# Cross-attention on one core: the score products split into column halves

## The chip, the cores and the metric

The kernel runs on one core of a Trainium2 chip. The metric is the device time of one execution in microseconds, from repeated executions on the same chip; the median is quoted. All data is 32-bit floating point.

The core has a matrix engine (PE in the profile, with PEld for the loads of its stationary operand), a vector engine (DVE), a scalar engine (ACT), a general engine (POOL) and a queue that issues transfers (SP). A product on PE holds up to 128 columns of one operand still in the array (the stationary operand, `lhsT`) while the columns of the other (the moving operand, `rhs`) stream past. The result lands in an accumulation memory, the PSUM, and several products can be summed there: the first has `start=True`, the last `stop=True`.

## The reference

For each of 64 batch items, `x` is 256 x 512 and `ctx` is 256 x 384:

```
text_p  = x   @ W_text  + b_text           # 256 x 512
audio_p = ctx @ W_audio + b_audio          # 256 x 512
Q = layer_norm(text_p,  g1, beta1)
K = layer_norm(audio_p, g2, beta2)
scores = Q @ K.T / sqrt(512)               # 256 x 256
alpha  = softmax(scores, axis=-1)
H = (alpha @ audio_p) @ W_out + b_out
out = layer_norm(H + x, g_out, beta_out)   # 256 x 512
```

The scores are the part that the change touches: 256 queries by 256 keys, each a sum over 512 hidden values.

## The kernel before

The work is staged as a software pipeline over the 64 items. The order of the instructions on each engine is the order in which the program text emits them; there is no scheduler. In one turn of the main loop (62 turns, `for b in range(B - 2)`) the kernel makes, in this order on PE: the scores of item `b`; the query projection of item `b + 2` (`ps_q`); the context product of item `b - 2`, or `alpha @ ctx` (`ps_z`); the key projection of item `b + 2` (`ps_k`); the output projection of item `b - 2` (`ps_y`). The projections use a scheme with seven block products instead of eight (class `Blocks`, line 487), so their moving operands are 256 columns wide as well. The last two items are finished after the loop in a shorter order, where the probabilities are turned on PE (`ps_e`, line 575) and the output is made with 512 columns (`ps_y`, line 639).

For the scores (method `scores` of class `Attention`, line 526), `qT` holds the normalised queries with the hidden dimension on the partitions, in `HC` = 4 chunks of 128; `kT` holds the keys in the same form. `LT` = 2 blocks of 128 queries are made one after the other. For each block, four products are summed into one 128 x 256 region of the PSUM tile `ps_sc`: the stationary operand is a 128 x 128 piece of `qT`, the moving operand is the 256-column chunk of `kT`. That is 8 products for an item.

Each product of 32-bit data stands in the trace as two pairs of records, a load of the stationary operand (LDWEIGHTS, on PEld) and the product itself (MATMUL, on PE): 64 items of 8 products are 1024 records of each kind for line 526. A transposition on PE (lines 183, 214, 227, 575) has 128 columns and stands as one pair.

Before the scores, ACT scales and shifts `qT` and `kT` chunk by chunk (method `affine`, line 458); the first product on each chunk waits for it. After them, DVE takes the row maxima from the whole of `ps_sc` (line 536) and ACT makes the exponentials from it (line 543).

Of the kernel before, what the change touches and what calls it, by code (L numbers as in the profile page):

```python
# [15 lines left out]
P = 128  # L16
# [6 lines left out]
def kernel(  # L23
# [41 lines left out]
    nc = tc.nc  # L65
    ctx.enter_context(tc.manual_schedule())
    B, L, D = x.shape
    S, DA = c.shape[1:]
    H = w_text.shape[1]
    LT, ST = L // P, S // P  # L70
    DC, AC, HC = D // P, DA // P, H // P
# [442 lines left out]
    class Attention:  # L514
# [4 lines left out]
        def scores(self, end=False):  # L519
            if end:  # L520
                self.sc = p_pj.tile([P, LT, S], F32, tag="pj", name="ps_sc")
            else:
                self.sc = p_at.tile([P, LT, S], F32, tag="at", name="ps_sc")
            for t in range(LT):
                for k in range(HC):
                    nc.tensor.matmul(  # L526
                        self.sc[:, t, :],
                        lhsT=self.qT[:, k, bass.ts(t, P)],
                        rhs=self.kT[:, k, :],
                        start=(k == 0),  # L530
                        stop=(k == HC - 1),
                    )

        def maxima(self):
            self.nmx = small.tile([P, LT], F32, tag="nmx", name="nmx")
# [239 lines left out]
    q, k, xT, cT = {}, {}, {}, {}  # L775
# [319 lines left out]
```

## Time and profile before

| what | value |
|---|---|
| median of 3 runs | 1415.37 us (1414.96 to 1416.03) |
| span of the profiled execution, first to last instruction | 1411.8 us |
| PE busy | 1403.2 us, 99% of the span, 6437 records |
| PEld busy | 1220.4 us, 86%, 6437 records |
| DVE, ACT, POOL busy | 87%, 66%, 62% |
| score products on PE (line 526) | 1024 records of 128x256, 231.5 us busy |
| loads for them (line 526) | 1024 records of 128x128, 194.6 us busy |
| mean granted clock of PE | 0.999 |

For the profiled execution only the span is on record as its own time; the timed runs' median lies 3.6 us above it.

How to read it: a MATMUL record runs from the moment in which the engine begins to fetch to a modelled end, so records of neighbouring products overlap and the mean duration of a record (379 ns for 256 columns) is not what a product costs in a stream. What it costs there is the distance between the starts of two neighbouring records, which is called the pitch below. The chain of waits shows this: it merges a run of records of one line into one piece, and the piece's length over the number of records is the pitch. A busy time in the groups is the union of the records' times, put down to each group once.

### The profile page before, as it was taken

To read this page: it belongs to the slowest core of one execution; us is meant where nothing else is said; L and a number is where in the kernel's file an instruction comes from. 1 tells how busy PE (TensorE), PEld (TensorE's weight loads), DVE (VectorE), ACT (ScalarE), POOL (GpSimd) and SP (SyncE) were. 2 spreads that over 40 slices of the span, in tenths; PEclk is the share of its full clock that TensorE was granted. 3 is DMA by queue.
4 is the path that set the end of the run, shared out by engine and by line. 5 is a ranking of instruction groups with operands and counts; after the bars stand their busy time and mean duration, and the time that the engine had idled before them with its cause. 6 is when DMAs were issued, how large, how long until landed. Compare 5 with 4: busy or idle time off the path is not lost.

```text
span 1411.8 us, 22761 instructions
## 1 busy us (share of the span) xinstructions
PE 1403.2 (99%) x6437; PEld 1220.4 (86%) x6437; DVE 1230.4 (87%) x1758; ACT 935.0 (66%) x2298; POOL 871.0 (62%) x1294
## 2 busy tenths in 40 slices
PE   9999999999999999999999999999999999999998
PEld 5888888888888888888888888888888888888885
DVE  6888898898888988988988889889889888898887
ACT  4667667676676676676766766766767667667663
POOL 5556666656656666666566566666665665666645
PEclk9999999999999999999999999999999999999999
DMA  8798877888888887787887887877888888878763
GB/s 211 206 259 229 245 233 218 246 232 224 241 243 219 232 233 228 234 226 237 231 230 235 225 238 232 231 232 232 221 243 237 222 240 239 222 235 232 223 212 125
DMA packets 450437, 322.32 MB, mean 228 GB/s; under 512 B 154885, under 2 KB 382981, under 8 KB 450310
## 3 DMA queue, kind: packets, MB, share of 16 engines
q1 hardware_dynamic: 450214, 320.72, 80.3%
q8 instruction: 52, 0.85, 0.3%
q14 instruction: 75, 0.61, 0.2%
q10 hardware_dynamic: 96, 0.13, 0.0%
HBM read 203.83 MB, written 116.92 MB: 227 GB/s over the span
## 4 chain that ended last, share of the span: by engine, by line
PE 98%; DVE 1%; POOL 1%; DMA 0%; ACT 0%; issue 0%; DVEq 0%; ACTq 0%
PE ps_q L487 27%; PE ps_k L487 21%; PE ps_y L487 20%; PE ps_sc L526 15%; PE ps_z L592 12%; PE ps_wao L252 1%; PE ps_y L639 1%; PE ps_q L374 0%; PE ps_k L374 0%; DMA c<-in_ctx_dram 0%; DVE yr L499 0%; PE ps_rows L214 0%; POOL yr L608 0%; POOL x L772 0%; DVE kr L499 0%; PE ps_wa L227 0%
## 5 line engine op out<-in xcount | busy, mean ns | idle before, releaser
L499 DVE TENSOR_TENSOR qr<-ps_q,qr 128x512 f32<-128x512 f32 x252 | 174.3, 692 | 88.9 <-PE ps_q L487 86.1
L526 PE MATMUL ps_sc<-kT,qT 128*128 128x256 f32 x1024 | 231.5, 379 | 0.0
L353 POOL TENSOR_SCALAR ve<-var 128x2 f32<-128x2 f32 x126 | 43.4, 344 | 290.0 <-ACT junk L392 289.8
L526 PEld LDWEIGHTS ps_sc<-kT,qT 128*128 128x128 f32 x1024 | 194.6, 190 | 26.9 <-issue 0.5
L543 ACT ACTIVATE e<-ps_sc,nmx 128x256 f32<-128x256 f32 x128 | 59.4, 468 | 230.3 <-DVE nmx L536 230.3
L608 POOL TENSOR_TENSOR yr<-yr,x 128x512 f32<-128x512 f32 x124 | 155.7, 1277 | 70.8 <-DVE yr L499 70.8
L499 DVE TENSOR_TENSOR kr<-ps_k,kr 128x512 f32<-128x512 f32 x252 | 174.4, 692 | 22.5 <-DVE kr L499 0.9
L487 PE MATMUL ps_q<-wtsum,xsum 128*128 128x256 f32 x756 | 193.7, 379 | 0.0
L499 DVE TENSOR_TENSOR yr<-ps_y,yr 128x512 f32<-128x512 f32 x248 | 171.6, 692 | 21.7 <-DVE yr L499 0.5
L487 PE MATMUL ps_k<-wa,cT 128*128 128x256 f32 x630 | 177.1, 379 | 0.0
L592 PE MATMUL ps_z<-eT,c 128*128 128x256 f32 x768 | 176.2, 379 | 0.0
L487 PE MATMUL ps_y<-wao,zT 128*128 128x256 f32 x620 | 174.1, 379 | 0.0
L355 POOL TENSOR_TENSOR rstd<-ve,nhalf 128x2 f32<-128x2 f32 x192 | 157.3, 819 | 16.0
L592 PEld LDWEIGHTS ps_z<-eT,c 128*128 128x128 f32 x768 | 145.9, 190 | 20.3 <-issue 0.5
L487 PEld LDWEIGHTS ps_q<-wtsum,xsum 128*128 128x128 f32 x756 | 143.6, 190 | 19.5
L458 ACT ACTIVATE qT<-qT,columns 128x256 f32<-128x256 f32 x256 | 133.0, 593 | 4.1 <-DVE qT L91 4.0
L458 ACT ACTIVATE kT<-kT,columns 128x256 f32<-128x256 f32 x256 | 132.2, 588 | 2.3 <-DVE kT L91 1.3
L487 PEld LDWEIGHTS ps_k<-wa,cT 128*128 128x128 f32 x630 | 119.6, 190 | 16.2
L487 PEld LDWEIGHTS ps_y<-wao,zT 128*128 128x128 f32 x620 | 117.7, 190 | 16.0
L420 ACT ACTIVATE kr<-kr,rstd 128x512 f32<-128x512 f32 x126 | 84.0, 714 | 71.6 <-POOL rstd L355 71.6
L392 ACT ACTIVATE junk<-kr 128x512 f32<-128x512 f32 x126 | 79.4, 630 | 77.9 <-DVE kr L499 73.5
L487 PE MATMUL ps_q<-wt,xT 128*128 128x256 f32 x504 | 129.0, 379 | 0.0
(160 smaller groups left out, 2976.3 us busy)
## 6 DMA issues: line engine op xcount, KB each, us to landing
kd<-kr SPq DMA_DIRECT2D x64, 512.0 KB, 3.1
kq<-kd SPq DMA_DIRECT2D x256, 128.0 KB, 3.4
qd<-qr SPq DMA_DIRECT2D x64, 512.0 KB, 4.8
qq<-qd SPq DMA_DIRECT2D x256, 128.0 KB, 3.3
xq<-in_x_dram SPq DMA_DIRECT2D x252, 128.0 KB, 3.0
x<-in_x_dram SPq DMA_DIRECT2D x63, 512.0 KB, 4.3
out_dram<-yr SPq DMA_DIRECT2D x62, 512.0 KB, 4.8
cq<-in_ctx_dram SPq DMA_DIRECT2D x252, 96.0 KB, 2.5
```

What stands on the lines that cost most here:

```text
L252: nc.tensor.matmul(ps, lhsT=waT[k][:, bass.ts(a, P)], rhs=wo_sb[:, k, :], start=(k == 0), stop=(k == HC - 1),)
L353: nc.gpsimd.tensor_scalar(ve, var, EPS, None, ALU.add)
L355: nc.gpsimd.tensor_tensor(r, ve, nhalf[:, :n], ALU.pow)
L392: nc.scalar.activation(junk, self.rows[:, t, :], AF.Square, scale=1.0 / math.sqrt(H), accum_out=self.var[:, t : t + 1],)
L420: nc.scalar.mul(row, row, self.r[t])
L458: nc.scalar.activation(self.T[:, k, :], self.T[:, k, :], AF.Identity, bias=bet[:, k : k + 1], scale=gam[:, k : k + 1],)
L487: nc.tensor.matmul(place, lhsT=side, rhs=w, start=(i == 0), stop=(i == len(pairs) - 1))
L499: add = lambda o, i0, i1: nc.vector.tensor_tensor(o, i0, i1, ALU.add)
L526: nc.tensor.matmul(self.sc[:, t, :], lhsT=self.qT[:, k, bass.ts(t, P)], rhs=self.kT[:, k, :], start=(k == 0), stop=(k == HC - 1),)
L543: nc.scalar.activation(self.e[:, t, :], self.sc[:, t, :], AF.Exp, bias=self.nmx[:, t : t + 1], accum_out=self.den[:, t : t + 1],)
L592: nc.tensor.matmul(ps[:, j, :], lhsT=c_rows[self.b][:, s, bass.ts(lo + j, P)], rhs=self.eT[:, s, :], start=(s == 0), stop=(s == ST - 1),)
L608: nc.gpsimd.tensor_tensor(self.y[:, t, :], self.y[:, t, :], x_rows[self.b][:, t, :], ALU.add)
```

## The change

The keys' columns are taken in two halves of 128. For each block of queries and each half, the four chunks of the hidden dimension are summed into a 128 x 128 region of the same `ps_sc` tile. Each product has half the columns; there are 16 of them for an item instead of 8, and the 128 x 128 piece of `qT` is loaded for each. The chunk is still the innermost loop, so that neighbouring products have different stationary operands. The results and where they lie are the same; the tile, its pool, what reads it and the order on all other engines are not touched.

```diff
@@ -521,15 +521,17 @@
                 self.sc = p_pj.tile([P, LT, S], F32, tag="pj", name="ps_sc")
             else:
                 self.sc = p_at.tile([P, LT, S], F32, tag="at", name="ps_sc")
+            half = S // 2
             for t in range(LT):
-                for k in range(HC):
-                    nc.tensor.matmul(
-                        self.sc[:, t, :],
-                        lhsT=self.qT[:, k, bass.ts(t, P)],
-                        rhs=self.kT[:, k, :],
-                        start=(k == 0),
-                        stop=(k == HC - 1),
-                    )
+                for j in range(2):
+                    for k in range(HC):
+                        nc.tensor.matmul(
+                            self.sc[:, t, bass.ts(j, half)],
+                            lhsT=self.qT[:, k, bass.ts(t, P)],
+                            rhs=self.kT[:, k, bass.ts(j, half)],
+                            start=(k == 0),
+                            stop=(k == HC - 1),
+                        )
```

## The prediction

> **What bounds the kernel now.** I read the page's busy shares and chain first, then the chain inside one turn of the loop, then the rows on short products and their loads.
>
> ```profile
> span 1411.8 us, 22761 instructions
> ...
> PE 1403.2 (99%) x6437; PEld 1220.4 (86%) x6437; DVE 1230.4 (87%) x1758; ACT 935.0 (66%) x2298; POOL 871.0 (62%) x1294
> ...
> PE 98%; DVE 1%; POOL 1%; DMA 0%; ACT 0%; issue 0%; DVEq 0%; ACTq 0%
> ...
> L526 PE MATMUL ps_sc<-kT,qT 128*128 128x256 f32 x1024 | 231.5, 379 | 0.0
> ...
> L526 PEld LDWEIGHTS ps_sc<-kT,qT 128*128 128x128 f32 x1024 | 194.6, 190 | 26.9 <-issue 0.5
> ```
>
> PE makes 98% of the chain and has no idle time before any score product. The loads' group is what the change doubles: 194.6 us busy, each record 190 ns with some 26 ns between. The chain through one turn, in order of time (start, length, what):
>
> ```profile
> 700.02 4.75 PE ps_y L487 x22
> 704.76 3.45 PE ps_sc L526 x16
> 708.22 6.04 PE ps_q L487 x28
> 714.26 2.59 PE ps_z L592 x12
> 716.85 4.75 PE ps_k L487 x22
> ```
>
> A turn is 16 + 28 + 12 + 22 + 22 = 100 records, end to end on PE, with no other engine between. In the chain the query pieces of 28 records start at 82.30 and at 1312.55 us, 57 turns apart: 1230.25 / 57 = 21.583 us a turn, 215.83 ns a record. So anything added to the scores of a turn moves the end by as much, unless the turn has a gap that absorbs it, and there is none.
>
> What a short product costs is seen near the start, where products of 512 columns and transpositions of 128 stand side by side:
>
> ```profile
> 10.96 0.44 PE ps_rows L214 x4
> 11.40 0.86 PE ps_k L374 x2
> 12.26 0.44 PE ps_rows L214 x4
> 12.70 6.87 PE ps_q L374 x16
> 19.56 0.66 PE ps_wa L227 x6
> 20.22 0.43 PE ps_k L487 x2
> ```
>
> 6.87 / 16 = 429.4 ns for 512 columns (record by record, the starts lie 429.2 apart); 0.44 / 4 and 0.66 / 6 = 110 ns for 128 columns (record by record 109 to 110, mean 109.2). So the pitch is linear: (429.17 - 215.83) / 256 = 0.8333 ns a column, and 215.83 - 256 x 0.8333 = 2.5 ns that each record pays whatever its width. At 128 columns that gives 106.67 + 2.5 = 109.17 ns, as the transpositions show.
>
> How loads behave at such a pitch (first view: PEld in order of time; second: the records of the tile ps_k around the same place, durations as least/median/greatest):
>
> ```profile
> 19.95 0.30 PEld L487 LDWEIGHTS ps_k<-wa,cT 128*128 128x128 f32 x2
> ```
>
> ```profile
> L487 PE MATMUL ps_k<-wa,cT x2: 379/380/382, 20.1 to 20.3; 128*128 128x256 f32 x2
> ...
> L487 PE MATMUL ps_k<-wasum,csum x1: 382/382/382, 21.2 to 21.2; 128*128 128x256 f32 x1
> ```
>
> Two loads of full 32-bit weights of 190 ns each take 0.30 us together, so the second started 110 ns after the first: 190 ns is a record's length, not the room that a load needs. And the first full product behind a run of transpositions, the only one whose load has 109 ns instead of 216 to hide in, is 3 ns longer (382 for 379), as is its distance to the next.
>
> **The change part by part.** *Removed:* 1024 records of 256 columns at 215.83 ns; in one item 16 x 215.83 = 3453.3 ns. *Added:* 2048 records of 128 columns, 32 in an item, at a pitch p that no row shows for full products at this speed. *Its ends:* it can't be under the streaming alone, 106.67 ns, and is most likely not over 213.3 ns. The latter is the pitch of the only run of full products of 128 columns:
>
> ```profile
> L198 PEld LDWEIGHTS ps_ones<-ones x12: 287/333/333, 1.5 to 3.8; 128*128 128x128 f32 x12
> L198 PE MATMUL ps_ones<-ones x12: 421/421/581, 1.5 to 4.0; 128*128 128x128 f32 x12
> ```
>
> These run in the first 4 us, where the array goes at half speed although the clock reads 1.00 (transpositions there stand 213 ns apart too). Past the first, each starts 213.3 ns after the one before: 2 x 106.67, with the load of 333 ns fully hidden beside a product of the same width. So load and stream need about the same time and run beside each other; at half speed nothing is added, at full speed the fixed costs show.
>
> *The value I take.* With a load of its own for each 128 columns, the chain of one step is: a product starts, the next load starts some 2 ns later (19.946 and 19.948 in the records), the load needs about as long as the stream, the next product starts. The trace has 7 places where a full product follows a transposition at full speed. In each the next start comes 2 to 3 ns late: 218 for 215.83 in four, 432 for 429.17 in three; mean 2.5 ns, once more the fixed part of a record. So p = 109.17 + 2.5 = 111.67 ns, and I expect it at every score record, since every load now has only one short product to hide behind.
>
> *Sum.* 32 x 111.67 = 3573.4 ns, minus 3453.3, is +120.1 ns for an item. Of 64 items, 63 are on the path: the scores of the last but one (1373.68 us) lie beside a chain on DVE and POOL from 1369.6 to 1382.6, after which PE waits 0.37 us; that takes the 0.12. 63 x 0.120 = +7.6 us. On the profiled execution that is 1411.8 + 7.6 = 1419.4 us of span; the timed median lies 3.6 above its span, which I leave as it is: 1415.4 + 7.6 = 1423.0 us, +0.53%.
>
> *Waits that move.* The first half needs all four chunks of both operands within 8 short records, 0.9 us, instead of 1.7. In the steady turns ACT is done with `kT` 5.0 us before the scores start and with `qT` 6.9 us before, so nothing shows. Two items are closer. In item 1 the last chunk of `qT` is done at 57.55 us and its load would now start near 57.66 instead of 57.97. In item 63 `kT` is done 0.1 us before the scores start. I cost both at nothing, at most 0.2 us. DVE's maxima wait for the last product as before and come 0.12 us later in a turn, where ACT already waits 3.6 us on the mean (230.3 / 64) without PE waiting for ACT. Other engines get 0.12 us more in each turn. Transfers, the vector engine's work and PSUM buffers stay as they are.
>
> *Two rules against the trace.* The row is the pair of loads 110 ns apart with 2.5 ns of delay. Against it stands the Trainium skill, "TensorE: Matmul & The Clock Gate", section "Back-to-back issue gap": in a sustained stream of loads and products, 128 columns cost about 81 ns in 16-bit data, where a product by itself would need about 56, so a load that is not covered adds 25. By that rule p would be 134 and the sum +53 us; I estimate from the row, which is of this data type. "Perfetto Trace Analysis", section "Identifying the Most-Contended Engine", judges the engine by the busy share of its weight loads; read that way, 2048 loads of 190 ns are 389 us where the scores have 221 now, +168 us. The trace's overlapping load records speak against taking that share as occupancy.
>
> **The rivals.**
>
> 1. *The load hides fully.* The 2.5 ns may belong to the change from transposition to product. For it: at half speed no delay shows. Against: the same 2.5 ns at both widths and all 7 places. Then p = 109.17, 40.1 ns an item, +2.5 us: 1417.9.
> 2. *The handover costs more than at a single place.* A run of 32 short pairs may drain what is fetched ahead, or short sums into the same 128 PSUM columns may hold each other up; the longest run at full speed in the trace is 6 transpositions. At p = 115 it is +14.3 us, 1429.7; at 125, +34.4, 1449.8. Nothing in the rows asks for it.
> 3. *Loads in series.* If a load held its place for 190 ns, p = 192: +170 us, 1585. Two loads within 0.30 us and the 12 hidden ones speak against it.
> 4. *Faster.* If the fixed 2.5 ns vanished for short products, as the 213.3 at half speed could be read, p = 106.67, -40 ns an item: -2.5 us, 1412.9. It decides from p below 215.83 / 2 = 107.92; 0.2% faster needs 106.5, under the streaming itself. The transpositions at 109.2 speak against it.
> 5. *It does not do what it says.* If loads of the same queries were shared by the halves there would be half as many; but the chunk is innermost, neighbouring products differ in their queries, and PE's order shows 16 products of 128x128 where 8 of 128x256 stood, with nothing moved on any engine. No chance of its own.
>
> **How the numbers follow.** A measurement of this kernel can tell about 0.2% from no change, 2.8 us; with 63 x 32 records that is p above 109.3. Forecast (p 110.5 to 113): 0.68. Rival 1: 0.12; it lies within 0.2%, close to its edge, so I count 0.09 as same and 0.03 as slower. Rival 2: 0.15. Rival 3: 0.02. Rival 4 and what I do not see: 0.03, of which 0.01 as same. Slower is 0.68 + 0.03 + 0.15 + 0.02 = 0.88, same 0.10, faster 0.02. The range starts under rival 1, at 1417.4, and goes to p = 115.5 (+15.3 us), 1430.7, which takes in the cheap part of rival 2; the rest of it, rivals 3 and 4, are left out.
>
> **What the next profile would show.** Line 526 with 2048 records each on PE and PEld; a piece of the chain "ps_sc L526 x32" of 3.57 us (3.49 for rival 1, 3.68 for p = 115); products of 275 to 276 ns instead of the 273 of a transposition, since the delay shows in a record's length; turns of 21.70 us; other groups unchanged. PEld busy would be less than 2048 x 190 ns, for the records overlap. The forecast is wrong if the piece is longer than 3.7 us, or if PE shows idle time ahead of score products, which would be a wait that I did not see.

## The result and the profile after

The changed kernel takes 1422.26 us (median of 4 runs, 1421.63 to 1422.84) against 1415.26 us before (4 runs): a ratio of 1.0049 with a 95% interval of 1.0033 to 1.0065, or +7.0 us (+4.7 to +9.2). Forecast were 1423.0 us and +7.6.

The page of the changed kernel, in the lines that answer to those shown of before:

```profile
span 1420.5 us, 24809 instructions
...
PE 1411.9 (99%) x7461; PEld 1255.0 (88%) x7461; DVE 1230.8 (87%) x1758; ACT 935.6 (66%) x2298; POOL 872.4 (61%) x1294
...
PE 98%; DVE 1%; POOL 1%; DMA 0%; ACT 0%; issue 0%; DVEq 0%; SPq 0%; ACTq 0%
...
L528 PEld LDWEIGHTS ps_sc<-kT,qT 128*128 128x128 f32 x2048 | 239.0, 192 | 4.2 <-issue 0.5
L528 PE MATMUL ps_sc<-kT,qT 128*128 128x128 f32 x2048 | 239.7, 275 | 0.0
```

PE and PEld have 1024 records more each; the other engines have as many instructions as before. 2048 loads of 192 ns would be 393 us one after another; their union is 239.0 us, so the records overlap. A product's record is 275 ns, where a transposition of the same width has 272 to 273. The loads' group had 26.9 us of gaps in the kernel before and now has 4.2 us: load records stand nearly end to end through the scores.

The chain through one turn (start, length, what):

```profile
704.76 4.75 PE ps_y L487 x22
709.51 3.57 PE ps_sc L528 x32
713.08 6.05 PE ps_q L487 x28
719.13 2.59 PE ps_z L594 x12
721.72 4.75 PE ps_k L487 x22
```

The scores' piece is 3.57 us for 3.45; the other pieces are as before to 0.01 us. From the start of item 3's scores to that of item 61's there are 58 turns; they take 21.7033 us each, where the same measure gives 21.5833 before. That is 120.0 ns more in a turn. Record by record, the starts of neighbouring score products lie 111 or 112 ns apart (the trace has whole nanoseconds), one time in three 111, so 111.67 on the mean. Only the second record of an item follows the first after 109 to 110.

### The profile page after: what moved, and what is told of

Its sections match the earlier page's. It is cut to its first block, busy times and chain, and to the rows that moved or that the text cites. A ratio compares the mean times of both kernels' runs of the same rounds, so it can differ in the third digit from the quotient of the medians.

```text
span 1420.5 us, 24809 instructions
## 1 busy us (share of the span) xinstructions
PE 1411.9 (99%) x7461; PEld 1255.0 (88%) x7461; DVE 1230.8 (87%) x1758; ACT 935.6 (66%) x2298; POOL 872.4 (61%) x1294
## 4 chain that ended last, share of the span: by engine, by line
PE 98%; DVE 1%; POOL 1%; DMA 0%; ACT 0%; issue 0%; DVEq 0%; SPq 0%; ACTq 0%
PE ps_q L487 27%; PE ps_k L487 21%; PE ps_y L487 20%; PE ps_sc L528 16%; PE ps_z L594 11%; PE ps_wao L252 1%; PE ps_y L641 1%; PE ps_q L374 0%; PE ps_k L374 0%; DMA c<-in_ctx_dram 0%; DVE yr L499 0%; POOL yr L610 0%; POOL x L774 0%; DVE kr L499 0%; PE ps_rows L214 0%; PE ps_wa L227 0%
## 5 line engine op out<-in xcount | busy, mean ns | idle before, releaser
L528 PEld LDWEIGHTS ps_sc<-kT,qT 128*128 128x128 f32 x2048 | 239.0, 192 | 4.2 <-issue 0.5
L528 PE MATMUL ps_sc<-kT,qT 128*128 128x128 f32 x2048 | 239.7, 275 | 0.0
```

The source lines that it names most:

```text
L528: nc.tensor.matmul(self.sc[:, t, bass.ts(j, half)], lhsT=self.qT[:, k, bass.ts(t, P)], rhs=self.kT[:, k, bass.ts(j, half)], start=(k == 0) ...
```

## The experiments

The theory: each record brings a load; the load starts about 2 ns after the product before it and needs 106.7 + 2.5 ns, so that a record takes at least some 111.67 ns (111.65 in the expectations below) however few columns stream past, and 0.8333 ns a column + 2.5 where that is more. The rivals: a fixed toll on each short record, or a price of the scores alone. The measured turns below are means over the same 58 turns as above.

### The scores in quarters

```diff
-            half = S // 2
+            half = S // 4
-                for j in range(2):
+                for j in range(4):
```

> The scores in quarters of 64 columns, 64 records in an item. Theory (a load needs 106.7 + 2.5 ns and starts 2 ns after the product before it, so no record can follow in less than about 111.65 ns however narrow it is): pitch 111.65, 64 x 111.65 - 3453.3 = +3692 ns an item, +236 us over 64 items, about 1651 us. Rival (each short record only pays 2.5 ns more on its own streaming): pitch 64 x 0.8333 + 5.0 = 58.3 ns, +280 ns an item, +18 us, about 1433 us.

Measured: 1650.6 us in one run. The chain at one item's scores:

```profile
718.77 7.09 PE ps_sc L528 x64
```

7.09 / 64 = 110.8 ns for half the columns, and 111 or 112 from record to record behind the first. A turn takes 25.277 us, 3.693 more than before, where the theory said 3.692. In place of a streaming price there is a floor: products of 64 columns cost as much as products of 128. One part of the theory does not hold here: a load starts 55 to 56 ns after the product before it, where it is 1 to 3 ns in halves. What is the same in both is the distance from load to load, 111 to 112 ns.

### Unequal pieces of 160 and 96 columns

```diff
-            half = S // 2
...
-                for j in range(2):
+                for lo, n in ((0, 160), (160, 96)):
                     for k in range(HC):
                         nc.tensor.matmul(
-                            self.sc[:, t, bass.ts(j, half)],
+                            self.sc[:, t, lo : lo + n],
...
-                            rhs=self.kT[:, k, bass.ts(j, half)],
+                            rhs=self.kT[:, k, lo : lo + n],
```

> The scores in pieces of 160 and 96 columns, as many records as with halves. Theory (pitch is the greater of 0.8333 a column + 2.5 and 111.65): 16 x (135.83 + 111.65) = 3959.7 ns, +506 ns an item, +32 us, about 1447 us; the 160 ones at 135.8. Rival (a fixed toll of 5.0 ns on each record): 16 x (138.33 + 85.0) = 3573.3, the same as halves, +7.6 us, about 1423 us.

Measured: 1447.3 us in one run; the item's scores in the chain:

```profile
721.71 3.93 PE ps_sc L528 x32
```

As many records as with halves, and 3.93 us instead of 3.57; the turn, 22.090 us, has +0.507 against the theory's 0.506. The 160-column records stand at 135 to 136 ns, as streaming asks. Of each eight 96-column ones, seven stand at 111 to 112 ns and not at 80.0 + 2.5. The first of the eight, whose load lay beside a wide product, has only 82 to 83 ns; the 29 ns come back behind the group, where one 160-column record has 165 ns for 136. The fixed toll is out: by it the pieces would have cost no more than the halves.

### Narrower loads

```diff
-                for j in range(2):
-                    for k in range(HC):
+                for r, cuts in ((0, ((0, half), (half, half))), (64, ((0, S),))):
+                    for lo, n in cuts:
+                        for k in range(HC):
...
-                            self.sc[:, t, bass.ts(j, half)],
-                            lhsT=self.qT[:, k, bass.ts(t, P)],
-                            rhs=self.kT[:, k, bass.ts(j, half)],
+                                self.sc[r : r + 64, t, lo : lo + n],
+                                lhsT=self.qT[:, k, t * P + r : t * P + r + 64],
+                                rhs=self.kT[:, k, lo : lo + n],
```

> The stationary operand has 64 queries instead of 128: for the lower 64 rows the keys come in halves of 128 columns, for the upper 64 rows in 256 columns, 32 + 16 records in an item. Theory (the delay is the load's own time, which shrinks with its columns): the 128-column records stand at 109.17 ns and are 272 to 273 ns long, 32 x 109.17 + 16 x 215.83 = 6946.7, +3493 ns an item, +224 us, about 1639 us. Rival (a handover toll whatever the load's size): pitch 111.65 and records of 275 ns, +3573 ns an item, about 1644 us; the pitch in the trace decides.

Measured: 1559.4 us in one run, 80 to 85 us under the two expectations. The mechanism and the sum must be read apart. The records of the tile, durations as least/median/greatest:

```profile
L529 PEld LDWEIGHTS ps_sc<-kT,qT x3072: 132/137/137, 43.8 to 1536.5; 128*64 128x64 f32 x192
L529 PE MATMUL ps_sc<-kT,qT x3072: 272/273/431, 43.8 to 1536.7; 128*64 128x128 f32 x128, 128*64 128x256 f32 x64
```

A load of 64 columns is 137 ns long where one of 128 has 190 to 192: 53 to 55 ns less. The 128-column products are back at 272 to 273 ns, and where they run alone their starts lie 109 to 110 ns apart. So the 2.5 ns of delay go with the load's size and are not a toll on every handover, as the theory asked. (These products also use 64 columns of the array in place of 128, which no run separates from the load's size; and no run shows how low the floor of such loads lies.) The transpositions fit: their loads are 138 to 143 ns long in the kernel before, and they stand at 109 ns.

The Trainium skill's "TensorE: Matmul & The Clock Gate", section "LDWEIGHTS (loading the stationary operand)", gives a load the time of its columns over 1.2 per ns. The estimate from that is 107 ns for 128 columns and 53 for 64, and the measured difference of 53 to 55 ns agrees.

The sum was wrong for another reason: products for the lower and for the upper 64 rows of the result ran at the same time. At 729.510 us a load for the upper rows starts 2 ns after one for the lower, its product at 729.512; the 128-column records go on at 109 ns beside the 256-column ones. A turn is 23.852 us, 2.27 over before instead of 3.49, so 1.22 us less than the sum. That is the gain net of a loss: from the last product ahead of these scores to their first, and from their last to the first behind them, starts lie 309 to 310 ns apart instead of 216.

### The context products in halves, the scores left whole

```diff
                 for j in range(n):
-                    for s in range(ST):
-                        nc.tensor.matmul(
-                            ps[:, j, :],
+                    for h in range(2):
+                        for s in range(ST):
+                            nc.tensor.matmul(
+                                ps[:, j, bass.ts(h, P)],
...
-                            rhs=self.eT[:, s, :],
+                                rhs=self.eT[:, s, bass.ts(h, P)],
```

> Scores as in the kernel before; instead the context products (ps_z) are made in halves of 128 columns, 24 records for 12 in an item. Theory (it is a matter of 128-column records with their own loads, not of the scores): 24 x 111.65 - 12 x 215.83 = +89.6 ns an item, +5.7 us, 1421 us. Rival (a price of the scores alone, such as their operands' chunks or their place in the turn): pitch 109.2, +30 ns an item, +1.9 us, 1417 us.

Measured: 1421.30 us median of 5 runs, a ratio of 1.0039 (1.0024 to 1.0053). In the chain:

```profile
711.79 3.45 PE ps_sc L526 x16
...
721.29 2.68 PE ps_z L593 x24
```

2.68 us for 24 records, again 111.67 ns each; a turn is 21.6733 us, +90.0 ns where the theory had 89.6. So the price is not one of the scores alone: 128-column products of this data type with their own loads pay it at another place with other operands.

### The same queries one after the other

```diff
                 for k in range(HC):
                     for j in range(2):
                         nc.tensor.matmul(
                             self.sc[:, t, bass.ts(j, half)],
                             lhsT=self.qT[:, k, bass.ts(t, P)],
                             rhs=self.kT[:, k, bass.ts(j, half)],
-                            start=(k == 0),
-                            stop=(k == HC - 1),
+                            start=True,
+                            stop=True,
                         )
```

> Halves again, but the two halves of one chunk follow each other, so that neighbouring products have the same stationary queries. Each product stands alone (start and stop on every one), so this kernel leaves out the sum over the four hidden chunks: only the last chunk's product is left in the scores. Theory (every product brings its load, whatever is in the array): 2048 loads, pitch 111.65, +7.6 us, about 1423 us. Rival (a load of what is there already costs less or is left out): half of the handovers at 109.17, 16 x 2.5 = 40 ns an item less, +5.0 us, about 1420 us, to be seen in the pitch; with halves of the loads left out, 1024 loads.

Measured: 1422.0 us in one run. The chain there:

```profile
709.21 3.57 PE ps_sc L528 x32
```

The turn is 21.7033 us, the changed kernel's to the tenth of a nanosecond. Neighbouring products with the same queries cost as much as with different ones, so the order of the halves makes no difference to the floor. Nor does summing: these products do not accumulate. Each product has two loads of its own, and the trace does not show whether both put the same values into the array; what a load costs that repeats the one before it stays open.

### Three runs on the waits in item 1

The changed kernel's profile showed something that I had costed at nothing: PE waited inside the scores of item 1. The chain there:

```profile
57.72 0.60 PE ps_sc L528 x4
58.31 0.01 issue
58.32 0.49 PE ps_sc L528 x2
58.81 0.01 issue
58.81 3.17 PE ps_sc L528 x26
```

From the first to the last record of that item it takes 4.15 us instead of 3.46: the chunks of `qT` come from ACT 0.49 us apart and set the pace. To tell whether the change makes this wait, the first two items were left whole, and both kernels were profiled again.

```diff
-            half = S // 2
+            pieces = 2 if self.b > 1 else 1
+            half = S // pieces
-                for j in range(2):
+                for j in range(pieces):
```

> Halves from item 2 on, the first two items as before. Theory: 62 items x 0.120 = +7.4 us, 1422.8 us, and in its profile no wait inside the scores of item 1, or one no longer than the transfers of that execution make it. Rival (the 0.7 us that PE lost inside the scores of item 1 in the profile of the changed kernel are a price of the change): 7.0 - 0.24 - 0.7, +6.1 us, 1421.5 us.

> The changed kernel once more. Theory: +7.6 us to the kernel before, turns of 21.70 us, 32 records in 3.57 us; the wait inside item 1's scores depends on when the first transfers of an execution land and may be anything from 0 to 2 us. Rival (the wait belongs to the change): the same two waits of about 0.2 to 0.3 us inside item 1 again.

> The kernel before once more, for a second profile of it. Theory: turns of 21.583 us; its start up to the first scores differs from the first profile's 42.86 us by some tenths of a us, as the first transfers land, and a wait at or inside item 1's scores may show here too. Rival (the kernel before never waits there): none, and a span of 1411.8 us again.

Measured: 1423.28 us (median of 4 runs, 1420.58 to 1424.05; ratio 1.0053, 1.0038 to 1.0068) from item 2 on, 1421.99 us (4 runs; ratio 1.0047, 1.0031 to 1.0064) for the changed kernel, 1415.95 us in one run for the kernel before. The times do not separate them; the traces do. The chain of the kernel before, in its second profile:

```profile
53.20 3.88 DMA qq<-qd
...
57.20 1.26 DVE qT L91
...
58.48 0.61 ACT qT L458
59.09 0.04 issue
59.14 3.90 PE ps_sc L526 x16
```

The untouched kernel also waits for `qT`, whose source `qq` had landed late, and 16 records take 3.90 us. The kernel split from item 2 on waited longer still: 1.8 us between two starts ahead of item 1's scores. Item 1's scores wait for `qT` in seven of the ten profiles, in three of them with that item's scores whole. So the wait can come without the change. It goes with the transfers of the execution: around it, DVE's longest wait for `qq` was 1.7 us in the changed kernel's first profile, 3.1 us in the second profile of the kernel before and 3.5 us in the kernel split from item 2 on. But what it costs once it is there is not the same in the two forms. This is the time from the end of ACT's last chunk of `qT` to the end of item 1's scores:

| kernel | last chunk done, us | scores done, us | behind it, us |
|---|---|---|---|
| before, second profile | 60.56 | 62.88 | 2.32 |
| halves, first profile | 58.76 | 61.82 | 3.06 |
| halves, second profile | 59.05 | 62.10 | 3.06 |
| halves, same queries together | 59.13 | 61.52 | 2.39 |

"Scores done" is the start of the last record plus one pitch (215.8 or 111.67 ns). The other two profiles with whole scores and a late item 1, of the context halves and of the kernel split from item 2 on, have 2.32 us as well. In halves with the chunk innermost, 26 of a late item's 32 records still lie behind the last chunk, 2.9 us of work; whole, 10 of 16, 2.2 us. With both halves of a chunk together it is 20 of 32, 2.2 us, and the time is nearly as before. An execution that is late there pays 0.74 us for the halving of its first two items, not the 0.24 of the sum.

## Why the prediction was right

- *What bounds the kernel.* PE end to end, no gap in a turn: the 120.0 ns show up in every turn and nothing absorbs them. This carried the forecast.
- *The pitch.* Taken as 111.67 ns from seven places where a full product follows a transposition 2.5 ns late; measured 111.67. In each item the second record follows the first after 109 ns, and the second query product behind the scores follows the first after 218, so the toll is shifted by one record and the sum is unchanged. The quarters, the unequal pieces and the narrow loads show that the price is a floor that goes with the load, and rule out a second fixed part on each record. The prediction's picture, in which each load starts 2 ns after the product before it, is right for halves and not in general: in quarters it starts 55 to 56 ns after, and the floor is the same. What all these runs share is the distance between loads.
- *The sum.* 32 x 111.67 - 3453.3 = 120.1 ns an item against 120.0. Times 63 it gives +7.6 us; the timed medians differ by 7.0 (4.7 to 9.2) in the first comparison and by 6.6 in the second, 1421.99 - 1415.42. That the total came so close is in part luck, for the two ends of the kernel were mis-sized. From the end of item 1's last chunk of `qT` to the end of the span, the second profile of the kernel before takes 1353.61 us and the two of the changed kernel 1361.77 and 1361.79. That is 8.2 us more: 0.74 for the first two items, 7.2 for the 60 turns from item 2 to item 62, 0.10 for item 62 and 0.12 for item 63. Yet the spans of these profiles differ by only 6.4 and 6.7 us, because that chunk was done at 58.8 and 59.0 us in halves and at 60.6 us in the kernel before. Whether the timed runs start as these profiles do, and whether the change moves that chunk, no run shows.
- *What lies around the span.* I left 3.6 us between the span of before and its timed median as lying outside. In every run with both on record the device time is 1.7 to 1.9 us above its own span. The other 1.8 us are most likely waits at the start that the first profiled execution was spared: the span of the second profile is 2.3 us longer, and all of it lies ahead of item 2's scores, which start at 81.01 us there and at 78.69 in the first. It does not touch the difference, which I took from the turns.
- *The item that absorbs.* I took item 62's scores as hidden beside a chain on DVE and POOL. That was a wrong reading: from its scores to those of item 63 it takes 14.19 us in both profiles of the kernel before and 14.29 to 14.30 in all four in which that item is in halves, so 0.10 of the 0.12 us come through. The scores feed that chain. DVE takes the row maxima, which wait for the last score product, ahead of the statistics `mvy`, and POOL's `ve` needs `mvy`. Before, `mvy` was done 5.95 to 5.96 us after the start of the scores, and `ve` followed the record ahead of it on POOL without a gap:

```profile
1379.81 0.64 POOL ve L353
```

In halves `mvy` is done at 6.07 us, and `ve` starts 24 to 40 ns after POOL is free. The changed kernel's chain:

```profile
1388.28 0.03 issue
1388.31 0.70 POOL ve L353
```

- *The waits that move.* Sized wrong. I gave items 1 and 63 at most 0.2 us. Item 63 did not wait. Item 1 lost 0.69 us between its first and last record in the first profile and 0.92 in the second, because I took `qT`'s finish in one good execution, 0.1 us early, as fixed. The step that failed is the reading of a single execution's slack: in the four profiles with item 1's scores whole, the last chunk was done at 57.6, 60.6, 61.2 and 62.6 us, and the forecast knew only the first. That reading also compared with the wrong record: the first load that needs the last chunk started at 58.18 us in the kernel before, and not at 57.97.
- *Rivals.* That the load hides fully (109.17) is out: 109 to 110 stands only behind an item's first record. A higher price of the handover did not come, with 32 or with 64 pairs in a row. Loads in series are out with the 239 us of union. Of the two rules of the Trainium skill, the one of "TensorE: Matmul & The Clock Gate", section "Back-to-back issue gap", led to an estimate of 134 ns for p, with the kernel 53 us slower; the trace has 111.67 for this data type. By the busy share of loads ("Perfetto Trace Analysis", section "Identifying the Most-Contended Engine") the scores would have cost 168 us more; PEld's share went from 86% to 88%.

## What to carry to other kernels

Read what a product costs from the distance between starts, and look for the floor that its load sets. Here, in 32-bit data and within a run of products with a load of 128 columns each, the distance was 111.67 ns on the mean for 64, 96 and 128 moving columns alike. So moving operands narrower than about 131 columns save nothing; that is an estimate, where 0.8333 a column + 2.5 reaches the floor. At 128 columns the halving costs only 3.5% of the split products' time. This kernel, which has no slack on PE, pays that in full; a kernel with slack was not tried. And a chunk that may arrive late is better used up before the next half starts: 2.39 us of work behind it instead of 3.06, though the one run with that order left out the sum over the chunks.

## What was not expected

Two products whose stationary operands have 64 columns, for different 64-row halves of the result, ran at the same time on PE without being asked to: loads started 2 ns apart and their products 6 ns, and a turn was 1.22 us shorter than the sum. A sum of pitches does not hold for such products. And in the first 6 us, where the granted clock reads 1.00, products and transpositions of 128 columns stand 213 ns apart that later take 109 to 112.
